# One pass for values and sums of two heads, a division in 32x32 blocks, and gates inside the routing's projection, in a decoder layer with a mixture of experts

## The chip, the cores and the metric

The kernel runs on one core of one Trainium2 chip. A core has five engines that work beside each other, each in the order of its own queue: TensorE (PE in the profile; PEld are its weight loads), VectorE (DVE), ScalarE (ACT), GpSimd (POOL) and SyncE (SP), which here only issues DMAs. They wait for each other by semaphores. The metric is the device time of one execution in microseconds (us); lower is better. The kernel before has a median of 1429.41 us in 3 runs (1425.82 to 1429.95).

## The reference, cut to what matters

The input x has 64 sequences of 128 rows of 128 elements, in fp32. Three residual steps follow each other; every one normalises its input first:

```
x = x + self_attention(layernorm(x))             # 16 heads of 8, 128 keys
x = x + cross_attention(layernorm(x), ctx, mask) # 16 heads of 8, 77 keys
x = x + experts(layernorm(x))                    # 8 experts, the best 2 of each row

# attention, for each head
p   = softmax(q k^T)            # max, exp, sum, division
out = p v

# routing, for each row
proj  = x Wp^T
gates = (proj / |proj|) (sim / |sim|)^T / temperature
top 2 of the gates, softmax over the two; out = sum of gate * expert(x)
```

Two things in it bear on the change. The softmax needs, beside the weighted values of a head, the sum of its exponentials. And a row's gates are a linear function of x, divided by the length of the row's projection.

## The kernel before

**Groups and steps.** All rows stay in SBUF (tiles xs). Four sequences make a group, so there are 16 groups, and each is one job of self attention and later one job of cross attention: 32 jobs, 128 sequences. The loop over s (L733) takes one sequence a step and has several sequences in flight: it computes the score tiles `ps` of sequence s, from which the maxima come, the turned score tiles `pt` of sequence s-4, from which the exponentials come, and the values of sequence s-5. A step has two halves (L740). Each half has, in this order: the score matmuls of two head groups of the one and two of the other sequence (`score_tiles`, L609), their maxima on VectorE (`maxima`, L645) and exponentials on ScalarE (`exps`, L671), one item of a list of other work (`next_`, L729), an item of the routing when it is due, a pass of `values` (L681), one scatter of routed rows, and one clearing.

The list of other work holds, for a job: the normalisation (GpSimd, `norm`), the turning of the normalised rows (`trans`, matmuls tp), the projections `query`, `key` and `value` (matmuls pq, pk, pv), for every second sequence `turn` (matmul pm: the maxima are turned and sent to a row of the query tiles, so that the turned scores come with the maximum subtracted), and `project` (L703, matmul py: output projection and residual add, and after a job's second one the statistics of the new rows and their inverse root on GpSimd).

**Values and sums.** Sixteen heads lie in 4 column groups c of 4 heads j. `values(z, False)` multiplies the exponentials of one sequence with the values, `values(z, True)` multiplies the same exponentials with columns of ones (`ones_w`), so that the sums of exponentials stand in the same 8 rows as the values of their head. Each pass has 16 matmuls, 4 heads accumulated into 32 rows for each of the 4 column groups. The values pass is in half 0 of a step, the sums pass in half 1. After the sums pass of every second sequence VectorE takes the reciprocal of the sums (L700, 128x256 elements) and multiplies (L701); the result aT is what `project` reads.

**Routing.** When a group has left cross attention, `route` (L249) puts five items on a list, due 2, 3, 4, 6 and 8 halves later (LATER, L26): `norm` (VectorE), `trans` (matmuls tp<-ident,x), `project` (matmuls pp with Wp; ScalarE squares them with a sum over the row, GpSimd makes the inverse root `rnorm` by a power and a Newton step, L151), `choose` (4 matmuls pg of the same rows with the gate matrix gT; VectorE multiplies with rnorm at L290 and then picks the two experts in some 20 small operations, to L319) and `place` (positions of the rows among their experts, by matmuls pr). Then 8 scatters of the group's rows go out on GpSimd's queue, one a half, each behind the newest exponential.

**Order.** TensorE runs in the order in which the code is written (L879). On the other engines the framework's scheduler puts the instructions in order, when it builds the program; a queue then runs strictly in that order.

**Buffers.** PSUM has 8 banks. In attention: `ps_m` 2 (all the other work), `ps_s` 2 (scores), `ps_t` 2 (turned scores), `ps_o` 2 (values and sums). A half's two score tiles take both banks of `ps_s`, so the score matmuls of the next half wait until the maxima of this one have been taken. In the expert stage, which follows attention: `ps_m` 2, `ps_h` 4, `ps_y` 2. There 78 tiles of 256 rows are fetched from DRAM, turned, multiplied by the weights of their expert, and stored; a last stage gathers the rows.

## Time and profile before

| | |
|---|---|
| median of 3 runs | 1429.41 us |
| the profiled execution | 1452.79 us, of it span 1451.1 us |
| TensorE matmuls, busy | 1238.6 us (85% of the span) |
| VectorE, ScalarE, GpSimd, busy | 758.4, 516.6, 578.7 us |
| self attention, a group of 4 sequences | 25.2 us (pq to pq, from 108.63 to 435.33 in 13 periods) |
| cross attention with routing, a group | 31.5 to 33.2 us (pq to pq, from 542.07 to 865.43) |
| first and last matmul ph of the experts | 1016.6 and 1381.6 us |

The profiled execution is 1.6% above the median of the runs; durations in the text are from it, and sums are made against its own time. The first 40 of its microseconds load and start, attention lasts until about 1000, the experts until about 1390. The span's view in 40 slices reads as follows; each digit is the busy share of one slice of 36 us in tenths, and PEclk is the clock that TensorE was granted:

```profile
PE 2789999999999999999999999985999997555930
...
DVE 3347666666766555655655657543533333333422
ACT 1034444444444343333343333331544442111410
POOL 5413424233342335555565654443300004666046
PEclk9579999999999999999999999997999999676975
```

TensorE is nearly always busy in attention, with VectorE at half to three quarters. But a matmul's end is modelled, so a busy TensorE row alone doesn't say that TensorE is what the kernel waits for: the chain that ended last has to be read too. In such a chain every piece is followed back to what released it. Rows of costly groups give busy time and mean duration, then the idle time of the engine in front of them and what ended it.

### The profile page before, as it was taken

The numbers are of one execution on the slowest core, as the hardware profiler recorded it, in microseconds if no ns is written. First come the engines' busy times: TensorE is split into PE (matmuls) and PEld (weight loads), VectorE is DVE, ScalarE is ACT, GpSimd is POOL, SyncE is SP. The second block draws the span as 40 slices with busy tenths as digits, with TensorE's granted clock in tenths as the row PEclk, the third lists the DMA queues.
The fourth block names the chain that finished last, engine by engine and source line by source line (L and its number), as shares of the span: only waits on it lengthen the run. The fifth ranks groups of instructions, "written<-read, shape, count | busy, mean of one in ns | idle before, by whom it ended". The sixth has DMA issues, their size and how long they took to land.

```text
span 1451.1 us, 47629 instructions
## 1 busy us (share of the span) xinstructions
PE 1238.6 (85%) x20147; PEld 1008.3 (69%) x20147; DVE 758.4 (52%) x2094; ACT 516.6 (36%) x1167; POOL 578.7 (40%) x928
## 2 busy tenths in 40 slices
PE   2789999999999999999999999985999997555930
PEld 1567777777777777777777777764999997444930
DVE  3347666666766555655655657543533333333422
ACT  1034444444444343333343333331544442111410
POOL 5413424233342335555565654443300004666046
PEclk9579999999999999999999999997999999676975
DMA  7542122121212112222221222101232222333222
GB/s 202 142 88 67 39 54 44 42 56 35 62 36 56 38 42 59 62 57 53 57 53 50 59 62 77 28 22 34 81 106 73 67 73 78 95 96 88 74 54 73
DMA packets 120214, 95.58 MB, mean 66 GB/s; under 512 B 22585, under 2 KB 102593, under 8 KB 120001
## 3 DMA queue, kind: packets, MB, share of 16 engines
q1 hardware_dynamic: 97328, 58.73, 16.4%
q0 software_dynamic: 8192, 16.79, 4.1%
q10 hardware_dynamic: 14480, 17.02, 3.9%
q8 instruction: 158, 2.59, 0.8%
q14 instruction: 56, 0.45, 0.1%
HBM read 49.60 MB, written 42.89 MB: 64 GB/s over the span
## 4 chain that ended last, share of the span: by engine, by line
PE 64%; POOL 12%; issue 9%; DVE 7%; DMA 4%; another core or an unknown queue 2%; ACT 1%; POOLq 0%; SPq 0%; ACTq 0%; DVEq 0%
PE po L692 13%; PE ps L631 12%; PE py L826 9%; PE ph L808 8%; PE pt L631 4%; PE pt L640 3%; POOL xn L170 3%; PE ps L640 3%; POOL rstd L154 3%; PE pq L569 2%; POOL r L860 2%; DVE m L650 2%; PE pk L581 2%; PE py L709 2%
## 5 line engine op out<-in xcount | busy, mean ns | idle before, releaser
L677 ACT ACTIVATE e<-pt 128x512 f32<-128x512 f32 (+1 forms) x512 | 277.3, 591 | 464.3 <-PE pt L640 211.2
L650 DVE TENSOR_REDUCE m<-ps 128x4 f32<-128x512 f32 (+1 forms) x512 | 274.8, 577 | 223.5 <-PE pt L631 91.1
L631 PE MATMUL ps<-kh,qh 31*128 31x128 f32 (+1 forms) x4096 | 335.3, 289 | 33.7 <-DVE x L170 10.9
L631 PEld LDWEIGHTS ps<-kh,qh 31*128 31x128 f32 x4096 | 282.1, 192 | 100.3 <-DVE m L650 31.1
L631 PE MATMUL pt<-qh,kh 32*128 32x128 f32 (+1 forms) x4096 | 323.2, 283 | 4.3 <-DMA qh<-md 4.1
L631 PEld LDWEIGHTS pt<-qh,kh 32*128 32x128 f32 (+1 forms) x4096 | 256.8, 166 | 6.0 <-issue 5.3
L860 POOL DMA_INDIRECT r<-yr,back x128 | 124.5, 973 | 256.4 <-DMA yr<-yr 203.5
L815 ACT ACTIVATE hT<-ph,wr 128x256 f32<-128x256 f32 x312 | 128.6, 470 | 237.8 <-issue 208.5
L365 POOL DMA_INDIRECT xr<-x,slot x128 | 129.8, 1014 | 162.6 <-ACT e L677 75.6
L808 PE MATMUL ph<-xT,wr 128*128 128x256 f32 x624 | 161.7, 405 | 29.2 <-issue 15.2
L826 PE MATMUL py<-wr,hT 128*128 128x128 f32 x1248 | 161.8, 281 | 25.8 <-issue 22.3
L826 PEld LDWEIGHTS py<-wr,hT 128*128 128x128 f32 x1248 | 158.2, 197 | 35.4 <-issue 25.7
L808 PEld LDWEIGHTS ph<-xT,wr 128*128 128x128 f32 x624 | 120.7, 204 | 46.4 <-issue 15.5
L700 DVE RECIPROCAL aT<-po 128x256 f32<-128x256 f32 x64 | 112.5, 1758 | 62.4 <-PE po L692 62.1
L692 PE MATMUL po<-e,vm 128*32 128x128 f32 (+1 forms) x4096 | 141.2, 277 | 1.4 <-issue 1.3
L692 PE MATMUL po<-e,ones_w 128*32 128x128 f32 (+1 forms) x4096 | 139.5, 277 | 0.0
L170 POOL TENSOR_SCALAR xn<-xs,stat,rstd 128x128 f32<-128x128 f32 x128 | 103.3, 815 | 82.6 <-PE tp L184 80.7
L692 PEld LDWEIGHTS po<-e,ones_w 128*32 128x32 f32 (+1 forms) x4096 | 104.8, 110 | 35.9 <-issue 26.7
L692 PEld LDWEIGHTS po<-e,vm 128*32 128x32 f32 (+1 forms) x4096 | 105.4, 110 | 28.8 <-issue 21.0
L832 DVE TENSOR_TENSOR yr<-py,wr 128x256 f32<-128x256 f32 x78 | 33.0, 423 | 171.3 <-PE py L826 136.1
L163 POOL TENSOR_SCALAR var<-stat 128x4 f32<-128x4 f32 x48 | 11.2, 233 | 246.8 <-DVE stat L149 244.0
L640 PE MATMUL pt<-ident_b,bias 128*77 128x512 bf16 x256 | 95.7, 391 | 0.0
(163 smaller groups left out, 1365.0 us busy)
## 6 DMA issues: line engine op xcount, KB each, us to landing
xr<-xr SPq DMA_DIRECT2D x78, 128.0 KB
yr<-yr SPq DMA_DIRECT2D x78, 128.0 KB
d<-qT ACTq DMA_DIRECT2D x32, 256.0 KB
qh<-d SPq DMA_DIRECT2D x128, 64.0 KB
xs<-in_x_dram SPq DMA_DIRECT2D x16, 256.0 KB
d<-kT ACTq DMA_DIRECT2D x16, 256.0 KB
kh<-d SPq DMA_DIRECT2D x64, 64.0 KB
we_s<-in_w_dram SPq DMA_DIRECT2D x16, 256.0 KB
```

The source lines that it names most:

```text
L170: (engine or nc.gpsimd).tensor_scalar(xn[:, b, :], xs[g][:, b, :], stat[:, i, 0:1], rstd[:, i : i + 1], ALU.subtract, ALU.mult,)
L365: i = nc.gpsimd.indirect_dma_start(out=part.x, out_offset=bass.IndirectOffsetOnAxis(ap=slot[:, g * GB + b, k : k + 1], axis=0), in_=v["xn" ...
L631: nc.tensor.matmul(pt[:, r, :], v[still][rows, r, b, :], v[moving][rows, r, b, :], start="bias" not in v or r == 0, stop="bias" not in v,)
L640: nc.tensor.matmul(pt, left, right.unsqueeze(1).to_broadcast([P, HG, K]), start=False, stop=True,)
L650: nc.vector.tensor_reduce(v["m", b // 2][:, c, :, b % 2], v.pop(("ps", b, c)), AX.X, ALU.max, negate=True,)
L677: i = nc.scalar.activation(e[:K], pt[:K], AF.Exp)
L692: nc.tensor.matmul(po[32 * c : 32 * c + 32, :], w[:, 32 * j : 32 * j + 32], v["e", b, c][:K, j, :], start=(j == 0), stop=(j == HG - 1),)
L700: nc.vector.reciprocal(r, v["o"][:, 1])
L808: nc.tensor.matmul(ph[:, c % 2, :], v["w"][:, c * P : (c + 1) * P], v["xT"], start=True, stop=True,)
L815: i = nc.scalar.activation(v["h"][:, n, :], ph[:, n % 2, :], AF.Gelu, bias=v["w"][:, WF + n : WF + n + 1],)
L826: nc.tensor.matmul(py[:, h, :], v["h"][:, c, h * P : (h + 1) * P], v["w"][:, F + c * D : F + (c + 1) * D], start=(c == 0), stop=(c == NFC ...
L860: inst = nc.gpsimd.indirect_dma_start(out=r, out_offset=None, in_=part.y, in_offset=bass.IndirectOffsetOnAxis(ap=back[:, i, k : k + 1], ax ...
```

## The change

**Values and sums together.** The tile of a head's values gets a ninth column of ones. A head's weights have 32 columns, of which the head needs 16 (8 values, the sum, zeros). The odd heads' weights start 16 columns earlier, so that a pair of heads fills 32 output rows with 16 each, and the two pairs go to different columns of the same bank. One pass of 16 matmuls then gives values and sums of all 16 heads; the pass in half 1 of each step is gone. Output columns are written in blocks of 32 queries with other blocks between them. `ps_o` has 1 bank in place of 2.

**Division in turned blocks.** After the pass of every second sequence VectorE turns the bank (128x512) in blocks of 32x32, so that values and sums of a head stand beside each other in a row, takes the reciprocal of 32 sums per partition, multiplies 256 elements, and turns the result back (128x256).

**Gates in the projection.** The gate matrix is put beside Wp as 8 more columns (wpg, 136 columns). The projection then gives the gates' raw values too; VectorE copies them out (raw). The matmuls pg are gone, and `choose` starts from raw. The projection takes two banks with two sequences each. `ps_m` has 3 banks, and `ps_h` 3 in place of 4.

**An order.** The routing's `norm` on VectorE is now put behind the newest maxima.

```diff
-    ps_m = ctx.enter_context(tc.tile_pool(name="ps_m", bufs=2, space=bass.MemoryType.PSUM))
+    ps_m = ctx.enter_context(tc.tile_pool(name="ps_m", bufs=3, space=bass.MemoryType.PSUM))
...
+    wpg = const.tile([P, D + E], F32, tag="wpg", name="wpg")
+    nc.scalar.dma_start(wpg[:, 0:D], wpT)
...
-        nc.vector.tensor_copy(gT, pg)
+        nc.vector.tensor_copy(wpg[:, D:], pg)
...
         def norm():
-            v["xn"] = normalised(g, "x3", 3, nc.vector)
+            with tc.issue_after(newest[1]):
+                v["xn"] = normalised(g, "x3", 3, nc.vector)
...
         def project():
-            pp = ps_m.tile([P, GB, D], F32, tag="mm", name="pp")
-            for b in range(GB):
-                nc.tensor.matmul(
-                    pp[:, b, :], v["xT"][:, b * S : (b + 1) * S], wpT_s, start=True, stop=True
-                )
             ssq = tiny("ssq", (P, GB))
-            for b in range(GB):
-                nc.scalar.activation(
-                    pp[:, b, :], pp[:, b, :], AF.Square, accum_out=ssq[:, b : b + 1]
-                )
+            v["raw"] = tiny("raw")
+            for h in range(2):
+                pp = ps_m.tile([P, 2, D + E], F32, tag="mm", name="pp")
+                for k in range(2):
+                    b = 2 * h + k
+                    nc.tensor.matmul(
+                        pp[:, k, :], v["xT"][:, b * S : (b + 1) * S], wpg, start=True, stop=True
+                    )
+                nc.vector.tensor_copy(v["raw"][:, 2 * h : 2 * h + 2, :], pp[:, :, D:])
+                for k in range(2):
+                    b = 2 * h + k
+                    nc.scalar.activation(
+                        pp[:, k, 0:D], pp[:, k, 0:D], AF.Square, accum_out=ssq[:, b : b + 1]
+                    )
             nc.gpsimd.tensor_scalar(ssq, ssq, 1e-24, None, ALU.max)
             v["rn"] = tiny("rnorm", (P, GB))
             inverse_root(v["rn"], ssq)
 
         def choose():
-            pg = ps_m.tile(full, F32, tag="mm", name="pg")
-            for b in range(GB):
-                nc.tensor.matmul(
-                    pg[:, b, :], v["xT"][:, b * S : (b + 1) * S], gT, start=True, stop=True
-                )
             gate = tiny("gate")
-            nc.vector.tensor_tensor(gate, pg, over_e(v["rn"]), ALU.mult)
+            nc.vector.tensor_tensor(gate, v["raw"], over_e(v["rn"]), ALU.mult)
...
-                t = heads.tile([P, GB * NG, HG, 32 + DH], F32, tag=f"vm{n}", name=f"vm{n}")
+                t = heads.tile([P, GB * NG, HG, 32], F32, tag=f"vm{n}", name=f"vm{n}")
                 nc.gpsimd.memset(t, 0.0)
+                nc.gpsimd.memset(t[:, :, :, DH : DH + 1], 1.0)
...
-                nc.vector.tensor_reduce(
+                i = nc.vector.tensor_reduce(
                     v["m", b // 2][:, c, :, b % 2], v.pop(("ps", b, c)), AX.X, ALU.max,
                     negate=True,
                 )
+                newest[1] = i.ins
...
-            def values(i, sums):
+            def values(i):
...
                 for j in range(HG):
+                    first = j % 2 == 0
                     for c in range(NG):
-                        w = ones_w[:K] if sums else v["v"][:K, b * NG + c]
-                        w = w.rearrange("p j w -> p (j w)")
+                        w = v["v"][:K, b * NG + c].rearrange("p j w -> p (j w)")
+                        at = 32 * j if first else 32 * j - 16
                         nc.tensor.matmul(
-                            po[32 * c : 32 * c + 32, :],
-                            w[:, 32 * j : 32 * j + 32], v["e", b, c][:K, j, :],
-                            start=(j == 0), stop=(j == HG - 1),
+                            v["o"][32 * c : 32 * c + 32, b % 2, :, j // 2, :],
+                            w[:, at : at + 32],
+                            v["e", b, c][:K, j, :].rearrange("p (n q) -> p n q", q=32),
+                            start=first, stop=not first,
                         )
-                if sums and b % 2:
-                    r = grp.tile([P, 2, S], F32, tag="aT", name="aT")
-                    v["aT", b // 2] = r
-                    nc.vector.reciprocal(r, v["o"][:, 1])
-                    nc.vector.tensor_tensor(v["aT", b // 2], v["o"][:, 0], r, ALU.mult)
+                if b % 2:
+
+                    n8 = 2 * S // 32
+                    t1 = grp.tile([P, n8, HG, 16], F32, tag="t1", name="t1")
+                    nc.vector.transpose(
+                        t1.rearrange("p n j w -> p (n j w)"),
+                        v["o"].rearrange("p b n r w -> p (b n r w)"),
+                    )
+                    r = grp.tile([P, n8, HG], F32, tag="r", name="r")
+                    nc.vector.reciprocal(r, t1[:, :, :, DH])
+                    t2 = grp.tile([P, n8, HG, DH], F32, tag="t2", name="t2")
+                    nc.vector.tensor_tensor(
+                        t2, t1[:, :, :, 0:DH],
+                        r.unsqueeze(3).to_broadcast([P, n8, HG, DH]), ALU.mult,
+                    )
+                    v["aT", b // 2] = grp.tile([P, 2, S], F32, tag="aT", name="aT")
+                    nc.vector.transpose(
+                        v["aT", b // 2].rearrange("p b q -> p (b q)"),
+                        t2.rearrange("p n j d -> p (n j d)"),
+                    )
...
-                    if z in range(NB):
-                        values(z, half == 1)
+                    if half == 0 and z in range(NB):
+                        values(z)
```

**The order that results.** In both built programs VectorE's queue in a routed cross group can be read off. Shortened to names, with m for one of a half's two maxima, and from the routing's norm on (before on the left, after on the right; the entries stand in queue order, and the columns are independent):

```
before                              after
norm of the routing (4)             norm of the routing (4)
m m  m m                            division (4 operations)
                                    m m
bias of the values, vm (4)          bias of the values, vm (4)
division (2 operations)             m m
m m  m m                            raw (2)
residual add, stats                 gate and all of choose
m m                                 m m
gate and all of choose              residual add, stats
m m                                 m m
division (2)                        division (4)
m m                                 m m  m m
place                               place
m m                                 m m
residual add, stats                 residual add, stats
                                    m m
```

Twelve of the sixteen routed groups have this order after the change; in the last four, which fall into the drain of attention, gate stands elsewhere. GpSimd's order from the normalised rows xn to the inverse root rnorm is the same in both programs.

More of the change, by code (lines that the diff above doesn't have):

```diff
@@ L68, in load @@
         return t
-    wq_s, wk_s, wv_s, wff_s, cq_s, ck_s, cv_s, co_s, wp_s, wpT_s = (
+    wq_s, wk_s, wv_s, wff_s, cq_s, ck_s, cv_s, co_s, wp_s = (
         load(w, [P, D], n)
@@ L73, in decoder_layer @@
             (wqT, "wq_s"), (wkT, "wk_s"), (wvT, "wv_s"), (wffT, "wff_s"), (cqT, "cq_s"),
-            (ckT, "ck_s"), (cvT, "cv_s"), (coT, "co_s"), (wp, "wp_s"), (wpT, "wpT_s"),
+            (ckT, "ck_s"), (cvT, "cv_s"), (coT, "co_s"), (wp, "wp_s"),
         )
@@ L108, in decoder_layer @@
     nc.gpsimd.tensor_copy(iom, ioi)
-    ones_w = const.tile([P, HG, 32 + DH], F32, tag="ones_w", name="ones_w")
-    nc.gpsimd.memset(ones_w, 0.0)
-    nc.gpsimd.memset(ones_w[:, :, 0:DH], 1.0)
     bqs_s = const.tile([P, 1], F32, tag="bqs_s", name="bqs_s")
@@ L226, in decoder_layer @@
     parts = [Part(0, 0, SPLIT), Part(1, SPLIT, NGRP)]
-    gT = const.tile([P, E], F32, tag="gT", name="gT")
+    wpg = const.tile([P, D + E], F32, tag="wpg", name="wpg")
+    nc.scalar.dma_start(wpg[:, 0:D], wpT)
     def gate_weights(work):
@@ L457, in table @@
         nc.vector.tensor_copy(back[:, every, :].rearrange("p b k -> p (b k)"), off)
-    last, newest, sending, clearing = {}, [None], [], []
+    last, newest, sending, clearing = {}, [None, None], [], []
     def behind(engine):
@@ L486, in attention @@
             tc.tile_pool(name="ps_t", bufs=2, space=bass.MemoryType.PSUM) as ps_t,
-            tc.tile_pool(name="ps_o", bufs=2, space=bass.MemoryType.PSUM) as ps_o,
+            tc.tile_pool(name="ps_o", bufs=1, space=bass.MemoryType.PSUM) as ps_o,
         ):
@@ L684, in values @@
                 K = S2 if jobs[n][0] else S
-                if b % 2 == 0 and not sums:
-                    v["o"] = ps_o.tile([P, 2, 2, S], F32, tag="o", name="po")
-                po = v["o"][:, int(sums), b % 2, :]
+                if b % 2 == 0:
+                    v["o"] = ps_o.tile([P, 2, S // 32, 2, 32], F32, tag="o", name="po")
                 for j in range(HG):
+                    first = j % 2 == 0
                     for c in range(NG):
-                        w = ones_w[:K] if sums else v["v"][:K, b * NG + c]
-                        w = w.rearrange("p j w -> p (j w)")
+                        w = v["v"][:K, b * NG + c].rearrange("p j w -> p (j w)")
+                        at = 32 * j if first else 32 * j - 16
@@ L884, in decoder_layer @@
             tc.tile_pool(name="ff", bufs=3) as ff,
-            tc.tile_pool(name="ps_h", bufs=4, space=bass.MemoryType.PSUM) as ps_h,
+            tc.tile_pool(name="ps_h", bufs=3, space=bass.MemoryType.PSUM) as ps_h,
             tc.tile_pool(name="ps_y", bufs=2, space=bass.MemoryType.PSUM) as ps_y,
```

## The prediction

> **What bounds the kernel now.** I read the page first (the chain and the costly groups), then the same chain in order of time inside one group of each attention stage, then the timelines of GpSimd (POOL) and VectorE (DVE) in one routed group.
>
> ```profile
> PE 64%; POOL 12%; issue 9%; DVE 7%; DMA 4%; another core or an unknown queue 2%; ACT 1%; POOLq 0%; SPq 0%; ACTq 0%; DVEq 0%
> ...
> L700 DVE RECIPROCAL aT<-po 128x256 f32<-128x256 f32 x64 | 112.5, 1758 | 62.4 <-PE po L692 62.1
> ...
> L692 PE MATMUL po<-e,ones_w 128*32 128x128 f32 (+1 forms) x4096 | 139.5, 277 | 0.0
> ```
>
> The change aims at the last two rows. But the chain is only 64% TensorE, and 12% POOL. The next view is the chain in one self group (one period of 25.2 us):
>
> ```profile
> 242.67 0.34 DVE xs L713
> ...
> 243.96 0.24 POOL var L163
> ...
> 248.78 0.21 POOL rstd L158
> ...
> 249.09 3.14 POOL xn L170 x4
> 252.24 0.04 issue
> 252.28 0.33 PE tp L184
> 252.61 1.01 PE po L692 x32
> ```
>
> From the end of the residual add (243.0) to the transpose of the next group's rows (252.3) no TensorE work counts: POOL makes two inverse roots and normalises. So over 9 of 25.2 us go no faster with fewer matmuls. The third and fourth views are a routed cross group, POOL and then DVE:
>
> ```profile
> 790.19 2.37 POOL L170 TENSOR_SCALAR xn<-xs,stat,rstd 128x128 f32<-128x128 f32 x3 [3.78 <-PE tp L184]
> ...
> 794.74 1.28 POOL L177 TENSOR_TENSOR xs<-xs,bo_s 128x512 f32<-128x512 f32 x1
> 796.11 0.24 POOL L279 TENSOR_SCALAR ssq<-ssq 128x4 f32<-128x4 f32 x1
> ...
> 798.39 0.20 POOL L158 TENSOR_TENSOR rnorm<-rnorm,newton 128x4 f32<-128x4 f32 x1
> ```
>
> ```profile
> 794.03 0.86 DVE L650 TENSOR_REDUCE m<-ps 128x4 f32<-128x308 f32 x2 [3.21 <-PE pt L640]
> ...
> 796.63 0.86 DVE L650 TENSOR_REDUCE m<-ps 128x4 f32<-128x308 f32 x2 [0.67 <-PE ps L640]
> 798.62 0.19 DVE L290 TENSOR_TENSOR gate<-pg,rnorm 128x32 f32<-128x32 f32 x1 [1.13 <-POOL rnorm L158]
> ...
> 801.63 0.20 DVE L319 TENSOR_TENSOR prob<-e,p 128x4 f32<-128x4 f32 x1
> 801.76 0.85 DVE L650 TENSOR_REDUCE m<-ps 128x4 f32<-128x308 f32 x2
> ```
>
> POOL starts when TensorE has turned xn (matmuls from 789.47) and delivers rnorm at 798.59, 9.1 us later; that distance is 9.11 or 9.12 in ten of the sixteen groups, and gate starts 0.03 after it each time. Then 3.2 us of small DVE operations run before the next maxima. The maxima of two halves, at 794.03 and 796.63, now stand ahead of gate.
>
> **The skill.** "VectorE: DVE Perf Modes", The three transpose paths, gives 311 ns for a VectorE transpose of 128x128 in 32x32 blocks; no run here shows one. "TensorEngine Tiling (Array Packing)", Key Properties, says that changing the tiling mode drains TensorE; the trace agrees: the first score matmul after a values pass waits 0.20 us for "issue" (404.84). "TensorE: Matmul & The Clock Gate", Part 1, says that an idle TensorE falls to half clock; here, after the gap of 941.3 to 945.2, a values pass takes 1.51 instead of 1.08 us. "PSUM — Partial Sum Buffer", Specifications, warns that non-contiguous patterns slow matmuls.
>
> **The change, part by part.**
>
> Sums pass: 128 passes of 1.01 us (252.61 to 253.62) and 16 of pg (0.8 us) leave TensorE: 142 us of work. What they are worth depends on what waits behind them.
>
> Division: reciprocal 1.76 and multiply 0.42, 2.2 us, against two transposes, a reciprocal of 32 and a multiply of 256 elements. The steps from 256 to 512 elements of PSUM input (0.42 to 0.68 us, L713 and L650) give 1.04 ns an element; with the skill's 311 ns the fixed part is 178 ns, so 0.71 and 0.44. The reciprocal: 1758 less 178, over 256, is 6.2 ns an element, so 0.37. The multiply like L713, 0.42. With gaps of 0.03: 2.0 us. Bounds 1.5 (everything at PSUM row rates with no gaps) and 3.2 (both transposes double). So the chain is hardly shorter, and it now stands a half earlier.
>
> Self group, walked by steps measured in the timeline from 404.8 to 412.4: next TensorE item 1.10 after a score group begins or 1.14 after the maxima that free its banks; two maxima 1.29, starting 0.09 after the scores; pq and pk 1.05, py 0.64, pm 0.22. From the score group after the xn transposes (before: 253.6) at 0: scores, py, done 1.74; maxima end 2.41; next item 3.55, pm, values, 4.78; maxima 3.65 to 4.94; next item 6.08, pq, 7.13; division 4.97 to 7.0; maxima to 8.3; next item 9.4, pk, values, 11.5; next item 12.6, maxima to 13.9 and then the add. Before, the same add begins at 14.3 (242.67 plus the period 25.2, less 253.6). Where the sums pass stood, TensorE now waits for maxima. Gain 0.3 a group, 13 periods between 109 and 435: -4 us.
>
> Routed cross group. The built program of the changed kernel has gate and all of choose directly behind the maxima of the half that projects (raw needs no later matmul), and ahead of the maxima of the next two halves. POOL's order up to rnorm is unchanged. So DVE blocks on rnorm, and behind it wait: two pairs of maxima, the py add, the stats; on ScalarE the choose exponential stands ahead of the next exps too. TensorE has two score banks and waits for those maxima. Steps, measured from 773.4 to 776.2: next item 1.77 after a score group begins, or 1.8 after what frees its banks; maxima from 1.40, a pair 0.86; exps end 0.93 after the next item. At 0 the xn transposes begin. Transposes and pp 1.4, values 1.0: 2.4. Scores, next item 4.2, py, 4.7. Gate 9.1, choose to 12.35, maxima to 13.25. Scores blocked until then: next item 15.05, and 15.95 at a cold clock (0.9 more, as 781.5 to 784.4 against the usual 1.8). pm and a cold values pass: 17.7. Scores and pq: 20.4. Division 17.8 to 19.85, maxima to 20.74: next item 22.5. pk, pr, values 24.5. Scores and py 26.8, exps end 27.2. Next item 29.0, pm, values 30.2. Scores, pv, x transposes 33.4. Meanwhile rstd comes 3.8 after the exps (as 776.16 to 779.93), at 31.0; the routing's norm, now behind the maxima, to 32.15; division to 34.2; maxima to 35.1; scores done 36.9. That is the period, against 324.3/10 = 32.4 before (transposes at 563.90 and 888.19).
>
> So the group loses 4.0 (sums) and about 0.9 (pg) of TensorE work and most of the former stall at the norm (2 us, DVE held for rstd ahead of the maxima), and gains a stall of 9.4: +4.5. Ten groups: +45. The first routed group (rnorm after 7.8) +3, the twelfth (5.7) +1. The last four routes, in the drain of attention, have rnorm without the xn work ahead; fewer sums against earlier gates: +2 (-4 to +8). Start-up before 109 us: -2.
>
> At nothing: ps_h with 3 banks (ScalarE is busy 21.8 of 50 us in the expert stage, 1050 to 1100; should a bank be late, it is at most one GELU of 0.47 a tile); ps_o with one bank (a whole step lies between a values pass and the next pair's first, the first transpose reads 0.7 us); ps_m with 3; the memsets and the weight load (start-up, beside loads). The values pass with scattered output keeps runs of 32 fp32, so I take 1.01; if that halves its speed, 2.0.
>
> Sum: -4+45+4+2-2 = +45 on the span of 1451.1, so 1496, and with the 1.7 around it 1498. The profiled execution is 1452.8 where the runs' median is 1429.41; scaled by 0.984: **1474 us**.
>
> **Rivals.** (a) Faster: rnorm is in time, or gate's wait falls where TensorE has cover. Then the blocked item is at 4.2+0.93+1.8 = 6.9 instead of 15.95, the period 27.9, -4.5 for 12 groups: -54, with the rest -58: 1372. For it: 142 us of matmuls leave the busiest engine. Against: POOL's 9.1 us and its order. (b) The stall costs 4 to 5 us less (no cold clock, POOL ahead by one scatter): no change, 1429. (c) Slower still: the scattered output doubles the values pass; 4 in each of 12 groups and 3 on the chain in 13: +87, 1560. For it the skill's warning, against it the long runs. The forecast itself turns on one place, gate in DVE's queue, its price is a us of period for each us of rnorm, and it decides for slower once rnorm comes over about 4.6 us after the xn transposes (9.1 less 4.5; 6 where a short stall leaves the clock warm). That the sums pass stays is excluded: the built program has none.
>
> **Numbers.** Forecast 0.77, (a) 0.13, (b) 0.05, (c) 0.05. Division bounds move it -12 to +35, cold clock and drain some 15. Range 1430 to 1520 leaves out (a) and (c), 0.18. About 0.3% is what a measurement of this kernel can tell from no change: faster 0.14, same 0.04, slower 0.82.
>
> **What would show it.** Right: idle of DVE before gate, released by POOL rnorm, of about 7 us in some 11 groups (before 0.03 to 1.13), routed periods of 35 to 38, self periods near 25, PEclk dips in every routed group. Wrong: gate starting without a wait, a division outside 1.5 to 3.2, a values pass well over 1.01, or self periods under 24.

## The result, and the profile after

The changed kernel takes 1499.31 us in the median of 4 runs (1494.35 to 1500.28), the kernel before 1429.68 beside it (1425.82 to 1432.43): a ratio of 1.0482, 95% interval 1.0448 to 1.0516. It is slower by 4.8%. The profiled execution is one of 1499.69 us, span 1497.9. From the page of its profile: two rows of the view in 40 slices, the shares of the chain that ended last, and one row of the costly groups:

```profile
PE   1878888888899977777777776889699999665940
...
PEclk9589999999999988788888888776699999788975
...
PE 53%; POOL 16%; DVE 13%; DMA 8%; issue 8%; ACT 1%; SPq 0%; DVEq 0%; POOLq 0%; ACTq 0%
...
L632 PE MATMUL ps<-kh,qh 31*128 31x128 f32 (+1 forms) x4096 | 385.7, 308 | 149.7 <-DVE m L651 130.5
```

TensorE lost two tenths of its busy share from the fifteenth slice on (524 us), where the routed groups begin, and its clock fell there too. In the chain TensorE's share went from 64 to 53%, that of VectorE rose from 7 to 13%. The last row says who holds TensorE: the score matmuls waited 130.5 us for maxima (in the kernel before the same matmuls waited 33.7 us in all, of which x ended 10.9).

One routed group shows where. The timeline of VectorE, changed kernel (start, duration, group, idle time ahead and what ended it):

```profile
675.22 0.86 DVE L651 TENSOR_REDUCE m<-ps 128x4 f32<-128x308 f32 x2 [0.66 <-PE ps L641]
...
684.72 0.19 DVE L289 TENSOR_TENSOR gate<-raw,rnorm 128x32 f32<-128x32 f32 x1 [7.39 <-POOL rnorm L154]
...
687.65 0.86 DVE L651 TENSOR_REDUCE m<-ps 128x4 f32<-128x308 f32 x2
...
693.76 0.72 DVE L704 STREAM_TRANSPOSE t<-po 128x512 f32<-128x512 f32 x1 [1.64 <-PE po L694]
694.51 0.35 DVE L709 RECIPROCAL r<-t 128x32 f32<-128x32 f32 x1
694.90 0.42 DVE L711 TENSOR_TENSOR t<-t,r 128x256 f32<-128x256 f32 x1
695.36 0.45 DVE L716 STREAM_TRANSPOSE aT<-t 128x256 f32<-128x256 f32 x1
695.73 0.83 DVE L651 TENSOR_REDUCE m<-ps 128x4 f32<-128x308 f32 x2
```

Gate waits 7.39 us for rnorm, and the maxima that it holds back come 12.4 us after those before them. The four rows from 693.76 to 695.36 are the new division: 2.05 us, to 695.81. The same group (36.93 us from one turning of xn to the next) in four stretches, busy time and granted clock, changed kernel:

```profile
core 0: us, PE busy (x) PEld busy (x) DVE busy (x) ACT busy (x) POOL busy (x), PEclk, DMA share, GB/s
675.59:680.44 4.85, 4.85 (x85) 4.05 (x83) 0.85 (x4) 2.78 (x11) 3.90 (x5) 1.00 0.02 5
680.44:688.18 7.74, 0.00 (x0) 0.00 (x0) 3.15 (x20) 1.17 (x3) 4.06 (x10) 0.66 0.03 8
688.18:693.70 5.52, 5.52 (x73) 4.08 (x74) 2.32 (x8) 1.32 (x3) 3.53 (x5) 0.55 0.16 41
693.70:712.52 18.82, 17.74 (x306) 13.78 (x307) 12.31 (x41) 7.35 (x15) 7.42 (x13) 1.00 0.32 80
```

In the second stretch TensorE does nothing at all for 7.74 us, and most of the third goes at half clock. The stages of the two profiled executions, from the starts of pq and ph:

| stage | before | after | difference | predicted |
|---|---|---|---|---|
| up to the fourth pq | 108.6 | 106.0 | -2.7 | -2 |
| self, 13 periods | 326.7 | 331.2 | +4.5 | -4 |
| three cross groups not routed | 76.0 | 69.2 | -6.9 | 0 |
| first routed period | 30.7 | 36.7 | +6.0 | +3 |
| ten routed periods | 323.4 | 377.8 | +54.4 | +45 |
| the next period | 34.4 | 38.9 | +4.5 | +1 |
| drain, to the first ph | 116.7 | 120.5 | +3.8 | +2 |
| experts and the end | 434.5 | 417.6 | -16.9 | 0 |

The last row isn't a gain of the change; the first experiment shows that.

### The profile page after: what moved, and what is told of

Same layout as the page of the kernel before. It is cut to its first block, busy times and chain, and to the rows that moved or that the text cites. A ratio compares the mean times of both kernels' runs of the same rounds, so it can differ in the third digit from the quotient of the medians.

```text
span 1497.9 us, 39257 instructions
## 1 busy us (share of the span) xinstructions
PE 1191.0 (80%) x15923; PEld 951.8 (64%) x15923; DVE 745.5 (50%) x2254; ACT 517.9 (35%) x1167; POOL 576.0 (38%) x929
## 3 DMA queue, kind: packets, MB, share of 16 engines
q1 hardware_dynamic: 97328, 58.73, 16.2%
q8 instruction: 125, 2.05, 0.6%
## 4 chain that ended last, share of the span: by engine, by line
PE 53%; POOL 16%; DVE 13%; DMA 8%; issue 8%; ACT 1%; SPq 0%; DVEq 0%; POOLq 0%; ACTq 0%
PE ps L632 13%; PE po L694 8%; PE py L844 7%; PE ph L826 7%; DMA r<-yr,back 6%; POOL xn L166 5%; PE pt L632 5%; DVE m L651 4%; PE pt L641 3%; PE ps L641 3%; POOL rstd L150 2%; POOL xr L364 2%; PE pk L582 2%; POOL r L878 2%; PE pq L570 1%
## 5 line engine op out<-in xcount | busy, mean ns | idle before, releaser
L632 PE MATMUL ps<-kh,qh 31*128 31x128 f32 (+1 forms) x4096 | 385.7, 308 | 149.7 <-DVE m L651 130.5
L632 PEld LDWEIGHTS ps<-kh,qh 31*128 31x128 f32 x4096 | 322.0, 209 | 244.2 <-DVE m L651 204.7
L632 PE MATMUL pt<-qh,kh 32*128 32x128 f32 (+1 forms) x4096 | 381.9, 305 | 5.4 <-DMA qh<-md 5.0
L632 PEld LDWEIGHTS pt<-qh,kh 32*128 32x128 f32 (+1 forms) x4096 | 303.4, 182 | 11.2 <-issue 6.5
L694 PE MATMUL po<-e,vm 128*32 128x128 f32 (+1 forms) x4096 | 158.1, 301 | 1.8 <-ACT e L679 1.7
L694 PEld LDWEIGHTS po<-e,vm 128*32 128x32 f32 (+1 forms) x4096 | 117.5, 120 | 40.0 <-issue 28.3
L641 PE MATMUL pt<-ident_b,bias 128*77 128x512 bf16 x256 | 107.6, 437 | 0.0
L883 DVE SCALAR_TENSOR_TENSOR xs<-r,prob,xs 128x128 f32<-128x128 f32 x128 | 44.2, 352 | 109.0 <-DMA r<-yr,back 108.5
L641 PE MATMUL ps<-bias,ident_b 128*128 128x308 bf16 x256 | 83.3, 331 | 0.0
L704 DVE STREAM_TRANSPOSE t<-po 128x512 f32<-128x512 f32 x64 | 45.7, 713 | 47.0 <-PE po L694 46.9
```

Source lines behind the costliest of these rows:

```text
L632: nc.tensor.matmul(pt[:, r, :], v[still][rows, r, b, :], v[moving][rows, r, b, :], start="bias" not in v or r == 0, stop="bias" not in v,)
L641: nc.tensor.matmul(pt, left, right.unsqueeze(1).to_broadcast([P, HG, K]), start=False, stop=True,)
L694: nc.tensor.matmul(v["o"][32 * c : 32 * c + 32, b % 2, :, j // 2, :], w[:, at : at + 32], v["e", b, c][:K, j, :].rearrange("p (n q) -> p n ...
L704: nc.vector.transpose(t1.rearrange("p n j w -> p (n j w)"), v["o"].rearrange("p b n r w -> p (b n r w)"),)
```

## The experiments

All ratios are to the kernel before, measured beside the run on the same chip. Its time there is the last column: it differs from chip to chip, so times from different chips aren't compared.

| run | ratio to before, 95% interval | self period | routed period | before, us |
|---|---|---|---|---|
| the changed kernel, first measurement | 1.0482 (1.0448 to 1.0516) | 25.7 | 37.8 | 1430 |
| the changed kernel again | 1.0431 (1.0408 to 1.0455) | 25.4 | 38.4 | 1459 |
| routing's part alone | 1.0792 (1.0744 to 1.0841) | 25.2 | 42.0 | 1455 |
| values and division alone | 1.0004 (0.9985 to 1.0023) | 25.5 | 33.9 | 1459 |
| gate behind the maxima | 0.9747 (0.9702 to 0.9792) | 25.4 | 31.0 | 1455 |
| gate a half later still | 0.9708 (0.9662 to 0.9754) | 25.5 | 30.8 | 1455 |
| rnorm ahead of xn | 1.0224 (1.0168 to 1.0280) | 25.5 | 35.6 | 1455 |
| roots of self a job ahead | 1.0228 (1.0198 to 1.0258) | 23.2 | 38.4 | 1459 |
| 26 unread matmuls | 1.0293 (1.0271 to 1.0315) | 25.7 | 37.2 | 1428 |
| 33 unread matmuls | 1.0316 (1.0273 to 1.0359) | 25.7 | 36.9 | 1460 |
| all orders, changed kernel | 0.9218 (0.9197 to 0.9239) | 23.3 | 27.4 | 1459 |
| all orders, kernel before | 0.9645 (0.9625 to 0.9666) | 24.4 | 29.3 | 1428 |
| all orders, and rnorm ahead of xn | 0.9359 (0.9324 to 0.9394) | 23.4 | 30.4 | 1460 |

Periods are in us, means over 12 self and 10 routed groups of one profiled execution (before: 25.2 and 32.3).

**The changed kernel again.** No edit.

> The changed kernel as it is, beside the kernel before on the chip of the other runs of this call. The kernel before took 1429 us in the first measurement and 1455 us beside the first four experiments, whose part of attention and experts has the durations of the first profile of before; the first profile of the changed kernel has an expert stage of 350 us (first to last ph) where that of before has 365. Theory (the chip differs, not the kernel): on one chip both take the same time in the expert stage, 364 to 366 us where the kernel before takes 1455, and the changed kernel about 1515 to 1525 us there, or 350 us and 1499 where it takes 1430; the ratio stays near 1.048. Rival (the change makes the expert stage 15 us faster, for instance by the PSUM banks): the expert stage takes 350 us also where the kernel before takes 1455, and the ratio falls below 1.04.

It took 1520.23 us beside 1458.91. Its expert stage, from the first to the last start of ph, took 372.0 us: as the 370.0 of before, not as the 355.0 of its own first profile. (The last ph of before starts at 1386.6, not at 1381.6; the 365 and 350 of the expectation are short by the same 5 us.) So the chip differs by some 17 us there, and no gain of the change shows in the expert stage. How well that is known: four of the kernels below, on one chip, took 369.1 to 374.2 us there, and the one of them with the PSUM banks of before took 369.1. The first theory holds.

**Gate behind the maxima.**

```diff
-            nc.vector.tensor_tensor(gate, v["raw"], over_e(v["rn"]), ALU.mult)
+            with tc.issue_after(newest[1]):
+                nc.vector.tensor_tensor(gate, v["raw"], over_e(v["rn"]), ALU.mult)
```

> The changed kernel with one order added: in VectorE's queue gate stands behind the maxima of the half before it may run, where it stood ahead of them, beside the transposes of the division. Nothing else differs. Theory (gate's place): VectorE no longer waits for rnorm in front of two pairs of maxima, TensorE's score groups are not blocked behind it and stay at the full clock; walking the steps gives a routed period of about 31.5 us in place of 37.8, so about 1430 us in place of 1499. Rival 1 (the loss comes from the division in turned blocks or from the values pass with its sums): the routed period stays above 36 us and the time within 10 us of 1499, since both are untouched. Rival 2 (the wait only moves: the maxima behind gate's new place are as urgent): the wait of VectorE for rnorm shrinks, but the period stays over 35 us, 1470 us or more.

The timeline of VectorE in this kernel:

```profile
678.15 0.86 DVE L652 TENSOR_REDUCE m<-ps 128x4 f32<-128x308 f32 x2 [0.60 <-PE ps L642]
680.21 0.19 DVE L290 TENSOR_TENSOR gate<-raw,rnorm 128x32 f32<-128x32 f32 x1 [1.20 <-POOL rnorm L154]
...
681.22 0.71 DVE L705 STREAM_TRANSPOSE t<-po 128x512 f32<-128x512 f32 x1
```

rnorm comes 9.11 us after the xn transposes, as before, but one pair of maxima now stands ahead of gate and only 1.2 us are left to wait. Most routed periods are 30.55. One line turns a loss of over 4% into a gain of 2.5%; division, values pass and banks are untouched, so both rivals fall. The gain is larger than expected, for the drain (104.1 us to the first ph, against 120.5 and 116.3 in the two profiles of the changed kernel) gains as well.

**Gate a half later still.** The same pin, and this:

```diff
-LATER = (2, 3, 4, 6, 8)
+LATER = (2, 3, 4, 7, 9)
```

> As the kernel with gate behind the maxima, and choose and place become due one half later (7 and 9 halves after the group has left, in place of 6 and 8), so that gate stands behind the next maxima and the division too, over 11 us after the xn transposes. Theory (gate's place): the wait for rnorm is gone altogether, the sums pass that was taken out is now worth its TensorE time; the walk gives a routed period of about 27.5 us, in all about 1385 to 1390 us, faster than the kernel before the change. Rival (POOL's chain of 9.1 us sets the period wherever gate stands): no faster than with gate one place later, 1430 or more. Rival (division or values pass cost the time): within 10 us of 1499.

The ratio came as expected (1385 to 1390 us of 1430 are 0.969 to 0.972), the period didn't: 30.8, not 27.5. So the agreement of the time is luck; the drain (103.0 us) and the groups ahead of these ten made up for them. In the routed groups it came as the first rival had it, hardly faster than with gate one place earlier (31.0), though for another reason than gate. Gate waits in three groups only, 6.5 us in all. But see the routing's norm in this kernel's timeline of VectorE:

```profile
666.05 1.15 DVE L166 TENSOR_SCALAR x<-xs,stat,rstd 128x128 f32<-128x128 f32 x4 [2.81 <-POOL rstd L154]
667.12 0.70 DVE L705 STREAM_TRANSPOSE t<-po 128x512 f32<-128x512 f32 x1
...
669.07 0.82 DVE L652 TENSOR_REDUCE m<-ps 128x4 f32<-128x308 f32 x2
```

The faster loop reaches norm before POOL has the root of the rows just finished: the wait moved from gate to x, 2.8 us in front of a division and a pair of maxima. In each routed group TensorE's clock is at half for 3.41 us or more.

**Routing's part alone.** Kernel before, with wpg, raw and the split projection of the change, without pg; `ps_m` 2, `ps_o` 2, sums pass and reciprocal kept:

```diff
-            nc.vector.tensor_tensor(gate, pg, over_e(v["rn"]), ALU.mult)
+            nc.vector.tensor_tensor(gate, v["raw"], over_e(v["rn"]), ALU.mult)
```

> The kernel before the change with the routing's part alone: gates as columns of the projection, choose from raw; the sums pass, the reciprocal of 256 elements, and all PSUM pools stay as before the change, and the routing's norm is not put behind the maxima. Theory (gate's place): gate moves ahead of the maxima of two halves as in the changed kernel and waits for rnorm, 9 us after the xn transposes, with all the sums passes still there; the routed period is 37.5 to 40 us against 32.5, in all about 1510 us, some 80 slower than before the change and not faster than the changed kernel. Rival (the loss comes from values, sums and division): this kernel is about as fast as before the change, 1420 to 1435 us, since it only drops 16 times 0.8 us of matmuls.

7.9% slower, more than the whole change; the direction is that of the theory, the size larger than expected (42.0 us a group, not 37.5 to 40). VectorE's timeline has the same wait with all sums passes in place:

```profile
660.96 0.19 DVE L291 TENSOR_TENSOR gate<-raw,rnorm 128x32 f32<-128x32 f32 x1 [6.75 <-POOL rnorm L158]
```

So dropping 0.8 us of matmuls a group cost 9.7 us of period: those matmuls stood behind two more score groups, and choose, which needed them, stood behind the maxima.

**Values and division alone.** The changed kernel with gT, pp and pg of the kernel before, and norm not pinned.

> The changed kernel with the routing of the kernel before: gT, the four matmuls pg in choose, pp with Wp alone, and no order for norm. One pass for values and sums, the division in turned blocks and the PSUM pools stay as changed. Theory (gate's place, a consequence of the routing's part): choose needs its matmuls again, so gate stands two halves later in VectorE's queue and hardly waits; self groups stay at 24.8 to 26.4, the routed period is about 31 to 32 us, and the time 0 to 2% below that of the kernel before. Rival (the values and division part costs time of its own): routed periods over 34 us and a time over that of the kernel before; with the routing alone at +8% and the whole change at +4.8%, parts that simply add would make this one 3% faster than before.

No difference in the whole: 1459.79 us against 1458.91, between theory and rival. But the routed period is 1.5 us longer than before; the three cross groups that aren't routed (69.2 us for 76.0) and the drain (110.3 for 116.7) gain. Gate waits 1.15 us, as before. TensorE's waits from 510 to 860 us, first the kernel before, then this one:

```profile
PE ps L631 <- DVE x L170: 9.6, 7, 1.4
PE ps L631 <- DVE m L650: 5.5, 4, 1.4
```

```profile
PE ps L630 <- DVE m L649: 40.1, 35, 2.4
```

(Total us, times, longest.) Without the sums pass TensorE stands where VectorE is held up: choose and the new division are interleaved in VectorE's queue, and the next maxima come 4.0 us after gate (670.11 to 674.11), where they came 3.1 after it (798.62 to 801.76). And the clock is at half for 13.7 us in every two routed groups, for 3.4 in the kernel before. The two parts don't add: +7.9 and 0.0 against +4.3 to +4.8. The whole has the pin on norm that neither part has; the pin alone was not tried.

**rnorm ahead of xn.** `inverse_root` hands out its last instruction (newest[2]), and the next group's normalisation is issued behind it:

```diff
-                    v["xn"] = normalised(g)
+                    with tc.issue_after(newest[2]) if newest[2] else nullcontext():
+                        v["xn"] = normalised(g)
```

> The changed kernel with POOL's order changed alone: the normalisation of the next group (xn, three tiles of about 0.8 us) is issued behind the routing's inverse root of the group before where it used to be ahead of it. Gate keeps its place ahead of the maxima. Theory (a us of period for each us of rnorm): rnorm comes about 5.3 us after the xn transposes in place of 9.1, VectorE's wait in front of gate shrinks by about 3.8 us, the routed period falls from 37.8 to about 33.5, in all about 1450 us. Rival (the wait at gate is a symptom and something else, the score banks or the cold clock, sets the period): rnorm comes earlier but the time stays within 10 us of 1499. Rival (the xn that is put off is late itself): the transposes of the next group wait for POOL instead, and the time is 1499 or more.

rnorm came 5.41 us after the transposes and gate waited 3.71 in place of 7.39, both as expected. But the period fell by 2.2 to 2.8, not by 3.7. From the release of the blocked score group to the next turning it took 27.9 us in one group (710.50 to 738.40) and 25.6 in the next (747.50 to 773.13), against 24.3 in the changed kernel (688.18 to 712.52). Half clock lasted from 708.9 to 722.5 in the first of them, 12.0 of its 13.7 us behind the release, and 5.7 us lay behind it in the second; in the changed kernel 5.3 of 10.2 us lay over idle time and only 4.9 behind the release. A us of rnorm is worth 0.6 to 0.8 us of period, not one.

**26 and 33 unread matmuls.** One more routing item, due in the half between project and choose:

```diff
-LATER = (2, 3, 4, 6, 8)
+LATER = (2, 3, 4, 5, 6, 8)
...
+        def fill():
+            pf = ps_m.tile([P, GB, D], F32, tag="mm", name="pf")
+            for k in range(26):
+                b = k % GB
+                nc.tensor.matmul(
+                    pf[:, b, :], v["xT"][:, b * S : (b + 1) * S], wpg[:, 0:D], start=True, stop=True
+                )
```

> The changed kernel with 26 more matmuls of 128x128 in each routed group, whose result nothing reads, put in TensorE's order behind py of the half in which VectorE waits for rnorm; TensorE had 7.7 us of idle time there, and they take about 7.0. Nothing is left out. Theory (part of the price of the wait is the half clock that the idle time brings: the score group after it took 3.9 us in place of 1.9 and the values pass 1.5 in place of 1.08): the clock stays full, the routed period falls by 2 to 3 us from 37.8 to 38.4, to about 35.5, and the time by 20 to 35 us, though TensorE does more. Rival (the clock is not what costs): periods and time stay within 0.5 us and 8 us of the changed kernel. Rival (TensorE's work is on the path there): the period rises by up to 7 us.

> As the run with 26 unread matmuls a routed group, with 33 of them. The 26 took 5.97 us and left TensorE idle for 1.95 us before the blocked score group; a half-clock stretch came all the same, 6.8 us long in place of 10.2 to 13.7, and the routed period fell only from 37.8 or 38.4 to 37.2. 33 should take 7.6 us and leave 0.3. Theory (the half clock follows even an idle time of 2 us, and its price is still in that run): no half-clock stretch in the routed groups, the score group after the wait takes 1.9 us, the period falls to 35 to 36 us, and the time 15 to 25 us below the run with 26. Rival (the half clock was cheap, and the rest of the period is maxima and waits): the period stays at 36.8 or more.

More work made the kernel faster, by 1.1 to 1.9 points, but on average the routed period hardly fell (with 26 matmuls 15 us of the 27.7 came from the drain). Single groups say more. With 26, some routed groups have no half clock and others 6.8 us of it. Two of them, from the release of the blocked score group to the next turning:

```profile
645.59:667.83 22.24, 21.16 (x375) 16.37 (x376) 14.54 (x49) 8.57 (x18) 10.95 (x17) 1.00 0.30 78
680.43:705.59 25.16, 24.07 (x374) 17.92 (x375) 14.75 (x49) 8.67 (x18) 10.95 (x17) 0.86 0.27 69
```

The same work takes 22.24 us at full clock and 25.16 with 6.83 us of half clock; other groups take 23.83 with 3.41 us and 26.73 with 10.24. So a us of half clock costs 0.43 to 0.47 us here. The kernel before shows it too. Its routed periods of 33.1 to 33.2 us have one stretch of 3.41 us at half clock each, those of 31.5 to 31.6 none:

```profile
606.72:639.86 33.14, 31.73 (x595) 25.52 (x594) 18.96 (x66) 12.55 (x31) 18.95 (x32) 0.95 0.21 55
639.86:671.38 31.52, 30.10 (x595) 24.14 (x595) 18.85 (x66) 12.53 (x31) 18.95 (x32) 1.00 0.23 58
```

And in the first profile of the changed kernel the same part of a group grows from 24.1 us, with 4.5 us of half clock in it, to 27.4 with 12.1 (0.43 us a us); in the second it grows from 24.7 with 3.7 to 27.2 with 10.3 (0.38). So the theory of the run with 26 holds where the clock does stay full: from turning to turning two such groups take 34.85 us each. From this an estimate of the two prices: 34.85 less the 31.5 of a group of before at full clock leaves 3.3 us for the wait, net of what the change saves (the unread matmuls lie inside the wait), and the other 2.1 of the 5.4 us that a routed group lost (37.8 less 32.3) are half clock.

With 33 the half clock is gone from the ten routed groups (one stretch of 3.4 us from 500 to 970, against 123 to 147 us), and yet the period is 36.9:

```profile
715.80:740.32 24.52, 22.30 (x375) 17.08 (x376) 14.48 (x49) 8.56 (x18) 10.95 (x17) 1.00 0.27 71
```

The rival's number came, but it doesn't show that half clock is cheap: at full clock this part takes 24.5 us here and 22.2 with 26. One score group takes 3.1 us (682.16 to 685.27) where it takes 1.9 with 26, and its matmuls have idle times between them marked "issue". The two ran on different chips, and the last experiment, on the chip of this one, shows the same. Whether the chip or the seven matmuls bring it stays open.

**Roots of self attention a job ahead.**

```diff
-                    if not cross:
-                        stats(g)
-                        root(g)
+                    if n == 0:
+                        stats(0)
+                        root(0)
                     v["xn"] = normalised(g)
+                    if n + 1 < NGRP:
+                        stats(n + 1)
+                        root(n + 1)
+                    while owed:
+                        root(owed.pop(0))
...
-                    root(g)
+                    if cross:
+                        root(g)
+                    else:
+                        owed.append(g)
```

> The changed kernel with one order changed in self attention: statistics and inverse roots of a group are computed one job ahead, the normalised rows come first in POOL's queue and the roots of the finished group after them; in the changed kernel two inverse roots and the normalisation stood in a row, about 9 us from the residual add to the transposes of the next group. Routing and cross attention stay as in the changed kernel. Theory (POOL's chain sets the self period, and TensorE waits there long enough for a half-clock window in every second group): the self period falls from 25.6 (24.8 and 26.4 in turn) to about 23, without half-clock windows in the self stage, so some 30 us less than the changed kernel; routed periods unchanged at 37.8. Rival (maxima and division on VectorE set the self period): it stays at 25 to 26, and the time within 10 us of the changed kernel.

23.2 us a group, no alternation, and 1491.42 against 1520.23 us on the same chip: as expected. In the changed kernel TensorE had waited at the turning for three of the four tiles of xn, 0.17 to 0.45 us each. Its stretches of 3.41 us around one such place:

```profile
297.17:300.58 3.41, 2.92 (x46) 2.25 (x42) 3.24 (x7) 1.67 (x3) 2.63 (x10) 1.00 0.43 55
300.58:303.99 3.41, 2.34 (x35) 1.53 (x36) 1.29 (x2) 1.08 (x2) 3.33 (x5) 1.00 0.02 5
303.99:307.40 3.41, 3.41 (x61) 2.93 (x64) 0.00 (x0) 0.59 (x1) 1.03 (x1) 0.50 0.03 5
```

TensorE was busy for 2.34 of 3.41 us and POOL for 3.33; the next stretch runs at half clock.

**All orders, on the changed kernel and on the one before.** The pin on gate, the roots a job ahead, and LATER = (3, 4, 5, 8, 10); for the kernel before also the pin on norm.

> The changed kernel with the roots of self attention computed a job ahead, gate pinned behind the newest maxima, and all five routing items one or two halves later (3, 4, 5, 8 and 10 halves after the group has left). In the run with gate two places later VectorE's wait moved from gate to the routing's norm, which stands in front of a division and two pairs of maxima and waits 2.8 us a group for POOL's root of the rows just finished; here it stands behind them. Theory (whatever waits for POOL in front of maxima costs its wait; without such waits the sums pass that was taken out is worth its TensorE time): routed periods of 27 to 29 us in place of 30.7, self periods of about 23, and a time about 6 to 8% below the kernel before. Rival (VectorE's own work, division, choose and maxima in one clump, sets the period by now): routed periods stay at 30 or more, and only the self stage gains, 4 to 5% below before.

> The kernel before the change, with all the orders of the fastest run so far and nothing of the change: roots of self attention a job ahead, routing items 3, 4, 5, 8 and 10 halves after the group has left, the routing's norm and gate pinned behind the newest maxima. The sums pass, the reciprocal of 256 elements and the matmuls pg stay. Theory (the sums pass is TensorE work that is worth its time once nothing waits for POOL): TensorE was busy for 24.16 of 25.21 us in a self group of the kernel before and for 30.9 of 32.4 in a routed one, so the orders alone can bring little: self periods of 24.2 to 25, routed of 31 to 32, 1 to 2% below the kernel before, against 7.8% for the same orders on the changed kernel. Rival (the orders did it all and the change is worth nothing): self near 23, routed near 27.5, 6 to 8% below before.

On the changed kernel 7.8% below before (1344.84 us beside 1458.91), the fastest of all, with 27.4 and 23.3 a group as the theory said. TensorE's waits from 510 to 860 us, the changed kernel and then this one:

```profile
PE ps L632 <- DVE m L651: 77.8, 18, 7.8
```

```profile
PE ps L639 <- DVE m L658: 8.2, 17, 2.6
```

On the kernel before the orders bring 3.5%, more than expected: the self groups came as said (24.4), the routed ones fell to 29.3. There TensorE is busy all the time (kernel before with the orders, one self and one routed stretch):

```profile
155.00:179.20 24.20, 23.80 (x538) 18.37 (x534) 17.48 (x38) 11.14 (x22) 8.09 (x17) 1.00 0.20 49
600.00:630.00 30.00, 30.00 (x606) 24.09 (x601) 18.91 (x66) 12.69 (x32) 19.53 (x32) 1.00 0.24 62
```

The expectation had taken TensorE's busy time in a routed group, 30.9 of 32.4 us, as a floor. Over a whole group of before at full clock it is 30.10 (the line 639.86:671.38 above), and the period went below that too, with the same matmuls. So a full row of TensorE isn't a floor; the ends of matmuls are modelled.

With the old orders the change costs 4.3 to 4.8%; with the new ones it saves 4.4% (0.9218 / 0.9645 = 0.956, the two ratios being from two chips).

**All orders, and rnorm ahead of xn.** The two edits together.

> The fastest run so far with the next group's normalisation put behind the routing's inverse root in POOL's queue, as in the run that did this alone. In the routed groups gate no longer waits, so nothing is to be gained there; in the last routes VectorE still waits 3.7, 3.3 and 2.9 us for rnorm. Theory (where no wait for POOL stands in front of maxima, POOL's order is worth nothing): within 0.5% of 0.922 of the kernel before. Rival (POOL's chain still sets part of the period): over 0.5% faster. Rival (the normalisation that is put off becomes late): over 0.5% slower, with TensorE's transposes of the next group waiting for POOL.

Slower by 1.4 points, the routed period 30.4: more than the theory allowed. The sign of the rival that forecast this isn't there: no wait of the transposes for POOL stands in the list of waits. In one group a score group took 5.1 us (715.35 to 720.45), its matmuls trickling with idle times marked "issue" while the DMA engines were 74% busy (716 to 718). Such idle times add up to 13.2 us ahead of score matmuls from 510 to 860 us, to 5.3 in the run without the edit. But the two ran on different chips, and the kernel with 33 unread matmuls, which leaves POOL's order alone, shows them on this chip too. So it isn't shown whether POOL's order or the chip costs the 1.4 points.

## Why the prediction was right, and where its sizes were off

Slower was predicted, at 1474 us in a range of 1430 to 1520; 1499 lies in it, 25 us above the forecast. The mechanism was the one forecast; the loss was put at 3.1% and is 4.3 to 4.8%.

**Gate in DVE's queue: right, and shown.** The idle time ahead of gate was to be about 7 us in some 11 groups: it is 7.39 or 7.40 in ten, 6.05 in the first and 3.70 in the twelfth. Moving gate alone shortens it to 1.2 us and takes the whole loss away.

**The walk of a routed group: right.** In the group shown, prob ended at 12.15 (12.35), the maxima at 12.9 (13.25), pm began at 16.2 (15.95), the division ended at 20.2 (19.85), and the next turning came at 36.93 (36.9). Six of the ten groups are like it. That the end fits so well is in part luck: the blocked scores began at 12.6, with the first of the two maxima, and not at 13.25, and from there to pm it took 3.65 us, not 2.7.

**"+4.5 in ten groups": mis-sized.** It measured +54, not +45. What was too small is the half clock: the walk took one length of it for all groups, 0.9 us at the blocked item and 0.4 in the values pass. Measured are 4.5 to 12.1 us of it behind the release, which at 0.43 us each make 1.9 to 5.2. Five of the twelve routed periods have one or two half-clock windows more and take 38.8 to 40.0. The last period and the first were put at +1 and +3 and measured +4.5 and +6.0. The +4.5 itself is the walk's 36.9 less 32.4; the four terms named beside it (-4.0, -0.9, -2, +9.4) make only +2.5.

**"Gain 0.3 a group" in self: right for half of the groups.** Periods of 24.8 alternate with 26.4: two are 51.2 us, fifteen windows of 3.41, and one window after a wait for POOL's xn falls to half clock. So -4 became +4.5. The trace of before had that wait too; with the sums pass beside it the clock had never dropped in that stage. That POOL's chain bounds a self group without its sums pass was right: taking it off brought 23.2.

**The price, "a us of period for each us of rnorm": too high,** 0.6 to 0.8 measured. In the first profile of the changed kernel 4.0 to 5.7 us of half clock lie over the wait in each of the ten groups; with rnorm earlier it is 1.0 to 1.7, and the rest lies over work. That accounts for a part of the difference; how large a part isn't shown.

**Division and values pass: right.** 0.71, 0.35, 0.43 and 0.45 us, a chain of 2.05 against 2.0; the figure for 128x128 from the Trainium skill ("VectorE: DVE Perf Modes", The three transpose paths; for bf16, these tiles are fp32) and the step of 1.04 ns an element gave 0.71 and 0.44. A values pass at full clock takes 1.08 us, as in the kernel before: runs of 32 fp32 didn't slow it, the warning in "PSUM — Partial Sum Buffer", Specifications, notwithstanding.

**Cross groups that aren't routed** were left out of the sum; they gain 2.3 us each (-6.9).

**The gap "of 941.3 to 945.2"** was misread: a sums pass runs until 942.4, and TensorE is idle for 2.83 us, not 3.9, before the clock falls at 946.7.

**The scaling by 0.984** put the profiled execution of before, 1452.8, down to 1429. It was rather one of the chips on which the kernel before takes 1449 us or more in every run: its expert stage takes as long as theirs. That the sum without the scaling, 1498, lies next to 1499 is luck, for it holds for another chip and a smaller loss. The difference ahead of the expert stage was +63.7 by the table, the medians differ by 69.6 on one chip and by 61.3 on the other.

## What to carry to other kernels

A matmul that is taken away may have been what kept a waiting instruction late in another engine's queue; after such a change read the new order of the strict queues and ask of each instruction that waits for a slow engine what stands behind it. Work taken off the busiest engine pays only when nothing that feeds it waits: here the same change was worth +4.3 to +4.8% or -4.4%, by the order of a few small items on VectorE and GpSimd. When one wait is gone, look for the next at once (gate, then x, then TensorE itself). And count the clock with the wait: a stall in TensorE's work costs its own time and then, in part, that of the half clock that follows.

## What the runs showed of the hardware

TensorE's clock falls without a whole idle window. "TensorE: Matmul & The Clock Gate", Part 1, of the Trainium skill speaks of at least one idle window of about 3.4 us. The windows of 3.41 us agree, but laid over the matmuls of the kernel before between 110 and 950 us, all eight drops follow windows in which TensorE was busy for 43 to 61%; in the changed kernel drops follow windows with up to 75%. The share isn't a sharp limit: windows with 52 to 69% also passed without a drop. In all fourteen profiles, from 100 to 1000 us, full clock came back only after windows of 93% or more, and not after every such window. The shares rest on modelled ends of matmuls.

A us of half clock over TensorE's work cost 0.43 to 0.47 us of time with 26 unread matmuls (22.24, 23.83, 25.16 and 26.73 us with 0, 3.41, 6.83 and 10.24 us of it), 0.48 in the kernel before (31.5 and 33.1 to 33.2 us, with 3.41), and 0.38 and 0.43 in the two profiles of the changed one.

One program takes 2% longer on some chips than on others: the kernel before 1428 to 1430 or 1455 to 1460 us, the changed one 1499 or 1520. In the profiles of the changed kernel 17 us of that are the expert stage (355.0 and 372.0).
